# Another order of loads and first projections in the opening of a two-layer kernel

## The chip, the cores and the metric

The kernel runs on one core of one Trainium2 chip. A core has a matrix engine (TensorE, PE in the profile), three engines for elementwise work (VectorE or DVE, ScalarE or ACT, GpSimd or POOL) and a synchronisation engine (SyncE or SP) that here only issues transfers. Each engine works through its own queue strictly in order; transfers from any queue share 16 DMA engines. Time is device microseconds, from the start of the program to its end; lower is better.

## The reference

Two pre-normed transformer layers over `x` of 2 sequences, 1024 tokens each, 128 channels, all in float32:

```python
x = x + _L0_attn_ref(_layernorm(x, axis=-1), L0_attn_Wq, ..., L0_attn_proj)   # 16 heads of 64, causal
x = x + _L0_ffn_ref(_layernorm(x, axis=-1), L0_ffn_W, ...)                    # dense + one of four low ranks
x = x + _L1_attn_ref(_layernorm(x, axis=-1), L1_attn_W_k, ...)                # 16 heads of 8, distances
x = x + _L1_ffn_ref(_layernorm(x, axis=-1), L1_ffn_Wr1, ...)                  # 8 experts, 2 used, + a shared one
```

The part that matters here is the way into the first attention:

```python
xn = (x - mean) / sqrt(var + eps)                     # per token
q = einsum('bse,hde->bhsd', xn, Wq) + bq              # k and v alike
scores = where(causal, -inf, q @ k^T / 8)
z = (softmax(scores) / 8) @ v
```

## The kernel before

The whole kernel is one function, `two_layers`. The first attention is cut into 16 units, one for each pair of heads of each sequence (8 chunks of 128 weight rows, for 2 sequences). `project(unit)` gives six pieces of work for a unit: q, k and v, each for two halves of 512 tokens. It reads the normed, transposed input `xnT` and the transposed weights `wqkvT`; a piece is two matmuls 64 wide over 512 tokens (q, k), or sixteen small ones (v), and an eviction from PSUM: q on ScalarE (L407), k on VectorE (L415), v on ScalarE (L423). After that a loop runs over 128 items of one query block each: `scores`, `weigh` (softmax), `divide`, `flip` (transposes), `keep`, `attend`, and in between the projections of the next unit. In the loop the order on the engines is the one written out by hand (`manual_schedule`); ahead of it a scheduler places the instructions, within the dependences and the buffers of the pools.

What stands ahead of the loop is called the opening here. In the order of the source it is this:

- `x` is loaded in four transfers of 256 KB on SyncE's queue (L77 and L78). 512 tokens each make a quarter; the first two are sequence 0.
- Wq and Wv are loaded whole (512 KB each) on ScalarE's queue, Wk on GpSimd's (L252 to L258). GpSimd's queue also carries the biases `bnat` and `vnat`, the output projection `proj` (512 KB), and some thirty small weights of the later parts (L260 to L303).
- `layernorm_T` (L115) takes the four quarters: statistics on VectorE (L121, L122), the reciprocal root through Ln and Exp on ScalarE (L99, L100) with a refinement on VectorE (L103 to L106), the normed tokens `xn` (L128), a transpose on TensorE (L132) and a copy to `xnT` (L133).
- The 24 chunks of the weights are transposed four at a time and copied to `wqkvT` (L307 to L312), then the biases.
- `small_weights` (L328) and `sides_of_rows` (L315) prepare the weights of the later parts: transposes with copies (L140, L141), a few small matmuls, and a chain at its end that goes over `wvT`, `bd`, two selects on GpSimd (L374, L378) and `m2` (L384).
- Then the PSUM pool of the opening is closed (`early.close()`, L732), the loop's pool is opened, and the six pieces of unit 0 are put out (L736).

PSUM has eight banks, and `dealt` shares them out. In the opening `big` gets four banks, which nothing there uses, `tr` (transposes) two and `acc` (projections) two. In the loop `acc` is a single bank:

```python
early.enter_context(dealt(big=(2, 2), tr=(2, 1), acc=(2, 1)))            # L249, the opening
l0.enter_context(dealt(sc=(2, 2), flip=(1, 2), z=(1, 1), acc=(1, 1)))    # L735, the loop
for piece in project(units[0]):                                          # L736
    piece()
```

A transfer issued by an engine's queue waits for the transfer that used the same semaphore before. There are eight semaphores for SyncE and ScalarE together, given out in the order in which the scheduler places the transfers, and eight for GpSimd; so a queue may stand still until an earlier transfer has landed, and everything behind it on that engine as well.

Of the kernel before, what the change touches and what calls it, by code (L numbers as in the profile page):

```python
# [9 lines left out]
FP = mybir.dt.float32  # L10
AF = mybir.ActivationFunctionType
ALU = mybir.AluOpType
AX = mybir.AxisListType

P = 128
# [5 lines left out]
def two_layers(ctx: ExitStack, tc: tile.TileContext, a: dict, out: bass.AP):  # L21
    nc = tc.nc
    V, S, G, T = nc.vector, nc.scalar, nc.gpsimd, nc.tensor

    B, SEQ, D = a["L0_attn_x"].shape
    H, DH, _ = a["L0_attn_Wq"].shape
    NC = H * DH // P
    NB = SEQ // P
    NT = B * NB
    TOK = B * SEQ  # L30
    NG = TOK // 512
# [10 lines left out]
    xnp = ctx.enter_context(tc.tile_pool(name="xnp", bufs=2))  # L42
# [5 lines left out]
    @contextmanager  # L48
    def dealt(waits="pool", **tags):
        assert sum(n * size for n, size in tags.values()) == 8  # L50
        with tc.tile_pool(name="ps", bufs=1, space=bass.MemoryType.PSUM, reuse_waits=waits) as pool:
            banks.update(pool=pool, tags=tags)
            yield
# [8 lines left out]
    def tr():  # L62
        return bank("tr").rearrange("p o (j q) -> p (o j) q", q=P)
# [10 lines left out]

    x = const.tile([P, NT, D], FP, name="x")
    xin = a["L0_attn_x"].rearrange("b (n p) e -> p (b n) e", p=P)
    for g in range(NG):  # L77
        nc.sync.dma_start(x[:, 4 * g : 4 * g + 4, :], xin[:, 4 * g : 4 * g + 4, :])  # L78

    nc.scalar.preload_act_table_set("natural_log_exp_and_others")  # L80
    ident = const.tile([P, P], FP, name="ident")
    make_identity(nc, ident)
# [29 lines left out]
            part()  # L112


    def layernorm_T():  # L115
        xnT = xnp.tile([P, TOK], FP, tag="xnT", name="xnT")
        for g in range(NG):
            mv = small.tile([P, 4, 2], FP, tag="mv", name="mv")
            for j in range(4):
                st = small.tile([P, V.BN_STATS_DIM], FP, tag="st", name="st")  # L120
                V.bn_stats(st, x[:, 4 * g + j, :])  # L121
                V.bn_aggr(mv[:, j, :], st)  # L122
            rstd = small.tile([P, 4], FP, tag="rstd", name="rstd")
            rsqrt(rstd, mv[:, :, 1], EPS, ALU.add)
            t = tr()
            for j in range(4):
                xn = work.tile([P, D], FP, tag="xn", name="xn")
                V.tensor_scalar(  # L128
                    xn, x[:, 4 * g + j, :], mv[:, j, 0:1], rstd[:, j : j + 1],
                    ALU.subtract, ALU.mult,  # L130
                )
                T.transpose(t[:, j, :], xn, ident)  # L132
            V.tensor_copy(xnT[:, bass.ts(g, 512)], t.rearrange("p j q -> p (j q)"))  # L133
        return xnT

    def transposed(dst, src):

        n, m = src.shape
        t = tr()
        T.transpose(t[:m, 0, :n], src, ident[:n, :n])  # L140
        V.tensor_copy(dst, t[:m, 0, :n])  # L141
# [85 lines left out]
    with ExitStack() as l0:  # L227
        wp = l0.enter_context(tc.tile_pool(name="l0w", bufs=1))
        wqkvT = wp.tile([P, 3, H * DH], FP, name="wqkvT")
# [16 lines left out]
        qkv = l0.enter_context(tc.tile_pool(name="qkv", bufs=3))  # L246
        zp = l0.enter_context(tc.tile_pool(name="zp", bufs=3))
        early = l0.enter_context(ExitStack())
        early.enter_context(dealt(big=(2, 2), tr=(2, 1), acc=(2, 1)))  # L249
        stage = early.enter_context(tc.tile_pool(name="stage", bufs=1))  # L250
        nat = []
        for i, k in enumerate("qkv"):  # L252
            w = stage.tile([P, NC, D], FP, name=f"nat_{k}")
            eng = (nc.scalar, nc.gpsimd, nc.scalar)[i]
            eng.dma_start(
                w, a[f"L0_attn_W{k}"].rearrange("h d e -> (h d) e").rearrange("(c p) e -> p c e", p=P)
            )
            nat.append(w)  # L258
        bnat = stage.tile([2 * NC, P], FP, name="bnat")
        for i, k in enumerate("qk"):  # L260
            nc.gpsimd.dma_start(
                bnat[i * NC : (i + 1) * NC, :],
                a[f"L0_attn_b{k}"].rearrange("(c two) d -> c (two d)", two=2),
            )
        vnat = stage.tile([H, 2, DH], FP, name="vnat")
        for r in range(2):
            nc.gpsimd.dma_start(vnat[:, r, :], a["L0_attn_bv"])
        nc.gpsimd.dma_start(proj, a["L0_attn_proj"].rearrange("(m p) e -> p m e", p=P))


        names = {
# [3 lines left out]
        raw = {}  # L275
        for k, src in names.items():
            raw[k] = stage.tile(list(src.shape), FP, name=f"raw_{k}")
            nc.gpsimd.dma_start(raw[k], src)
        raw["wd"] = stage.tile([NR, D], FP, name="raw_wd")
        raw["wu"] = stage.tile([P, P], FP, name="raw_wu")  # L280
        G.memset(raw["wu"], 0.0)
        for i in range(4):
            r = slice(roff[i], roff[i] + ranks[i])
            nc.gpsimd.dma_start(raw["wd"][r, :], a[f"L0_ffn_Wd{i}"])
            for j in range(2):
                nc.gpsimd.dma_start(
                    raw["wu"][:, j * DH + r.start : j * DH + r.stop], a[f"L0_ffn_Wu{i}"]
                )
        simI = stage.tile([NP, 4 + NP], FP, name="simI")
        nc.gpsimd.dma_start(simI[:, :4], a["L0_ffn_sim"])  # L290
        bp = stage.tile([NP, 1], FP, name="bp")
        nc.gpsimd.dma_start(bp, a["L0_ffn_bp"].unsqueeze(1))
        temp = stage.tile([P, 1], FP, name="temp")
        nc.gpsimd.dma_start(temp, a["L0_ffn_temp"].partition_broadcast(P))
        nc.gpsimd.dma_start(wr1, a["L1_ffn_Wr1"])
        nc.gpsimd.dma_start(br1, a["L1_ffn_br1"].unsqueeze(1))
        nc.gpsimd.dma_start(wr2, a["L1_ffn_Wr2"])
# [3 lines left out]
        nc.gpsimd.dma_start(raw["be1"][NE * NF :, :], a["L1_ffn_bs1"].rearrange("(f p) -> f p", p=P))  # L301
        nc.gpsimd.dma_start(be2[:NE, :], a["L1_ffn_be2"])
        nc.gpsimd.dma_start(be2[NE:, :], a["L1_ffn_bs2"].unsqueeze(0))  # L303
        xnT = layernorm_T()
        xn2T = xnp.tile([P, TOK], FP, tag="xnT", name="xn2T")

        for i in range(3):  # L307
            for c0 in range(0, NC, 4):
                t = tr()
                for c in range(4):  # L310
                    T.transpose(t[:, c, :], nat[i][:, c0 + c, :], ident)
                V.tensor_copy(wqkvT[:, i, c0 * P : (c0 + 4) * P], t.rearrange("p j q -> p (j q)"))  # L312
        transposed(bqk, bnat)

        def sides_of_rows():  # L315

# [73 lines left out]
        def project(unit):  # L390

            b, c = divmod(unit["n"], NC)
            q = unit["q"] = qkv.tile([P, NB, 2, DH], FP, tag="q", name="q")
            k = unit["k"] = qkv.tile([P, SEQ], FP, tag="k", name="k")
            v = unit["v"] = qkv.tile([P, NB, P], FP, tag="v", name="v", bufs=4)
            cols = bass.ts(c, P)

            def heads(which, xs):
                t = acc().rearrange("p j q -> p (j q)")
                for hh in range(2):  # L400
                    hs = slice(hh * DH, (hh + 1) * DH)
                    mm(t[hs, :], wqkvT[:, which, c * P + hh * DH : c * P + (hh + 1) * DH], xs)
                return t

            def do_q(j, xs):
                t = heads(0, xs)
                S.activation(  # L407
                    q[:, 4 * j : 4 * j + 4].rearrange("p i r u -> p i u r"),
                    t.rearrange("p (i u r) -> p i u r", r=2, u=DH),
                    AF.Identity, bias=bqk[:, c : c + 1], scale=-SC,  # L410
                )

            def do_k(j, xs):
                t = heads(1, xs)
                V.tensor_scalar(k[:, bass.ts(j, 512)], t, bqk[:, NC + c : NC + c + 1], None, ALU.add)  # L415

            def do_v(j, xs):
                t = acc()
                for i in range(4):
                    for half in range(2):  # L420
                        hs = slice(half * DH, (half + 1) * DH)
                        mm(t[hs, i, :], xs[:, i * P + half * DH : i * P + (half + 1) * DH], wqkvT[:, 2, cols])
                S.copy(v[:, 4 * j : 4 * j + 4, :], t)  # L423

            out = []
            for f in (do_q, do_k, do_v):
                for j in range(SEQ // 512):
                    xs = xnT[:, b * SEQ + j * 512 : b * SEQ + (j + 1) * 512]
                    out.append(lambda f=f, j=j, xs=xs: f(j, xs))
            return out  # L430
# [289 lines left out]
        for n in range(-1, len(units)):  # L720
            for i in range(4):
                if n >= 0:
                    items.append(units[n]["items"][4 + i])
                if n + 1 < len(units):
                    items.append(units[n + 1]["items"][i])
        transposed(bz, vnat.rearrange("h r d -> h (r d)"))
        V.tensor_scalar(bz, bz, SC, None, ALU.mult)

        V.tensor_scalar(bqk[:, :NC], bqk[:, :NC], -SC, None, ALU.mult)
        small_weights()  # L730
        sides_of_rows()
        early.close()  # L732
        pp = l0.enter_context(tc.tile_pool(name="pp", bufs=3))
        tp = l0.enter_context(tc.tile_pool(name="tp", bufs=1))
        l0.enter_context(dealt(sc=(2, 2), flip=(1, 2), z=(1, 1), acc=(1, 1)))  # L735
        for piece in project(units[0]):  # L736
            piece()
        zs = bank("z")[:, 0, :]
        longs, shorts, later, ends = [], [], [], []
        LAG = 2  # L740
# [647 lines left out]
```

## Time and profile before

| what | us |
|---|---|
| median of 3 runs | 1130.3 |
| lowest, highest | 1128.53, 1133.51 |
| the profiled execution | 1134.24 |
| its span | 1132.5 |
| PE busy in the span | 1033.1 (91%) |
| VectorE, ScalarE, GpSimd busy | 591.9, 679.9, 356.6 |
| VectorE's three waits for `x` in the first 40 us | 9.0 in all |
| first matmul of the program | 14.1 |
| first projection | 39.07 |
| first scores | 50.23 |
| first projection of unit 1 | 56.47 |

The profile is of one execution. Its page has the busy time of the engines, a row of busy tenths for each engine over 40 slices of the span with the clock that TensorE was granted, the chain of work that ended last, and groups of instructions. A group's line gives the source line, engine, operation, the written and read tiles, the count, then busy time with the mean of one in ns, and the idle time before them with what ended it. A float32 matmul is shown as two passes: two matmuls of a piece are "x4". PEld is TensorE's load of the standing operand. The shares of busy time are an average over the span, so the opening has to be looked at by itself: in its timeline, in stretches of some microseconds, and in the chain.

### The profile page before, as it was taken

What the parts mean: (1) busy time and instruction counts of PE and PEld (TensorE: products, weight loads), DVE (VectorE), ACT (ScalarE), POOL (GpSimd) and SP (SyncE); (2) the same over time, 40 slices, a digit from 0 to 9 for tenths busy, and PEclk for the clock granted to TensorE, in tenths of its full rate; (3) what the DMA queues carried; (4) which work ended last, traced back from release to release, by engine and by line L of the source; (5) the groups of instructions that cost most, each with busy time, mean ns of one, the idle gap of its engine ahead of it and who ended that gap; (6) DMA issues with size and microseconds to landing.
All of it is one profiled execution on the core that took longest, in us unless ns stands there. A gap on an engine that the chain in (4) does not pass through costs nothing.

```text
span 1132.5 us, 26027 instructions
## 1 busy us (share of the span) xinstructions
PE 1033.1 (91%) x10662; PEld 624.3 (55%) x10662; DVE 591.9 (52%) x1694; ACT 679.9 (60%) x1286; POOL 356.6 (31%) x496
## 2 busy tenths in 40 slices
PE   3699999999999999999778999999999997898798
PEld 2356766766666666767555233233333235698776
DVE  5366677787878788688753324012141114464432
ACT  1176666666766656676554777888784785334351
POOL 8133334343534443444441110000104002326513
PEclk9599999999999999999999999999998898789899
DMA  5000000000000000000005000000001000112112
GB/s 125 1 1 2 2 2 2 2 2 2 2 2 2 2 2 2 2 2 2 1 2 156 13 1 1 1 1 1 19 1 29 1 1 10 54 32 70 55 37 64
DMA packets 24358, 20.12 MB, mean 18 GB/s; under 512 B 2742, under 2 KB 21520, under 8 KB 24240
## 3 DMA queue, kind: packets, MB, share of 16 engines
q1 hardware_dynamic: 18352, 10.88, 3.2%
q0 software_dynamic: 3808, 6.53, 2.2%
q8 instruction: 84, 1.38, 0.5%
q10 hardware_dynamic: 2080, 1.05, 0.4%
q14 instruction: 34, 0.28, 0.1%
HBM read 13.34 MB, written 5.11 MB: 16 GB/s over the span
## 4 chain that ended last, share of the span: by engine, by line
PE 77%; DVE 9%; ACT 6%; issue 4%; POOL 1%; another core or an unknown queue 1%; DMA 1%; SPq 0%; DVEq 0%; ACTq 0%; POOLq 0%
PE accp L69 26%; PE bigp L69 13%; PE scp L69 10%; PE zp L69 9%; PE flipp L487 7%; PE upp L69 4%; PE trp L69 3%; ACT pT L492 2%; ACT p L457 1%; DVE pT L492 1%; DVE p L453 1%; DMA x<-in_L_attn_x_dram 1%; PE trp L1125 1%; ACT hs L1265 1%
## 5 line engine op out<-in xcount | busy, mean ns | idle before, releaser
L1097 ACT ACTIVATE e<-bigp 128x1024 f32<-128x1024 f32 x256 | 247.9, 1021 | 90.5 <-PE bigp L69 79.0
L469 POOL TENSOR_SCALAR p<-p,rz 128x128 f32<-128x128 f32 (+7 forms) x256 | 187.7, 746 | 305.5 <-DVE rz L466 270.8
L457 ACT ACTIVATE p<-p,nmax 128x128 f32<-128x128 f32 (+7 forms) x256 | 196.3, 769 | 25.1 <-DVE nmax L453 24.4
L453 DVE CUSTOM_DVE_ANT_0 p<-scp,mask 128x128 f32<-128x128 f32 (+7 forms) x256 | 183.4, 754 | 34.9 <-PE scp L69 24.6
L492 ACT COPY pT<-flipp 128x128 f32<-128x128 f32 (+7 forms) x128 | 81.3, 636 | 152.2 <-PE flipp L487 147.3
L69 PE MATMUL bigp<-rT,lT 32*128 32x512 f32 x1024 | 162.2, 649 | 4.8 <-ACT e L1097 4.4
L69 PE MATMUL scp<-k,q 64*128 64x512 f32 (+3 forms) x768 | 164.0, 509 | 0.0
L69 PEld LDWEIGHTS zp<-pT,v 128*64 128x64 f32 x2560 | 137.4, 138 | 26.2 <-issue 7.1
L69 PE MATMUL zp<-pT,v 128*64 128x128 f32 (+1 forms) x2560 | 147.3, 266 | 1.4 <-DVE zT L516 0.7
L487 PEld LDWEIGHTS flipp<-ident,p 64*128 64x128 f32 x2304 | 92.8, 140 | 98.6 <-issue 48.7
L69 PE MATMUL accp<-e,own 128*32 128x512 f32 x1024 | 141.4, 614 | 0.0
L487 PE MATMUL flipp<-ident,p 64*128 64x64 f32 x2304 | 112.0, 230 | 19.8 <-DVE rz L466 11.8
L492 DVE COPY pT<-flipp 128x128 f32<-128x128 f32 (+7 forms) x128 | 96.1, 751 | 59.0 <-PE flipp L487 59.0
L69 PEld LDWEIGHTS bigp<-rT,lT 32*128 32x128 f32 x1024 | 51.6, 185 | 115.4 <-issue 71.0
L973 POOL DMA_INDIRECT xs<-rows,from x46 | 46.9, 1020 | 189.2 <-PE trp L1245 87.6
L1265 ACT ACTIVATE hs<-upp,w 128x128 f32<-128x128 f32 x184 | 51.9, 371 | 73.9 <-issue 59.2
L69 PEld LDWEIGHTS scp<-k,q 64*128 64x128 f32 x768 | 70.0, 192 | 39.1 <-issue 34.2
L69 PE MATMUL accp<-xnT,wqkvT 128*64 128x512 f32 x256 | 72.5, 647 | 7.2 <-ACT q L407 2.8
L1114 DVE COPY cs<-accp 128x512 f32<-128x512 f32 x16 | 11.0, 690 | 105.4 <-PE accp L69 105.4
L69 PE MATMUL accp<-w,hs 128*128 128x128 f32 x368 | 54.7, 296 | 11.3 <-ACT hs L1265 8.6
L69 PE MATMUL upp<-xsT,w 128*128 128x128 f32 x368 | 56.4, 304 | 4.1 <-DVE xsT L1247 4.1
L69 PEld LDWEIGHTS accp<-e,own 128*32 128x32 f32 x1024 | 21.0, 108 | 68.7 <-issue 66.1
(313 smaller groups left out, 1152.5 us busy)
## 6 DMA issues: line engine op xcount, KB each, us to landing
given<-y SPq DMA_DIRECT2D x10, 256.0 KB, 2.3
wx<-in_L_ffn_We_dram SPq DMA_DIRECT2D x1, 2048.0 KB, 8.7
wx<-in_L_ffn_We_dram SPq DMA_DIRECT2D x8, 256.0 KB, 5.1
x<-in_L_attn_x_dram SPq DMA_DIRECT2D x4, 256.0 KB, 4.0
rows<-xn SPq DMA_DIRECT2D x4, 256.0 KB
out_dram<-out SPq DMA_DIRECT2D x4, 256.0 KB
xs<-rows,from POOLq DMA_INDIRECT x46
nat_q<-in_L_attn_Wq_dram ACTq DMA_DIRECT2D x1, 512.0 KB
```

The lines of the kernel that those rows point to most:

```text
L69: T.matmul(o, lhsT=lhsT, rhs=rhs, start=start, stop=stop)
L453: V.tensor_tensor_reduce(out=p[:, :n], in0=it["sc"][hh], in1=mask[:, SEQ - n :], scale=1.0, scalar=-NEG, op0=ALU.add, op1=ALU.min, accum_o ...
L457: S.activation(p[:, :n], p[:, :n], AF.Exp, bias=nmax, scale=-1.0, accum_out=it["sum"][:, hh : hh + 1],)
L469: G.tensor_scalar(p[:, :n], p[:, :n], r[:, hh : hh + 1], SC, ALU.mult, ALU.mult)
L487: T.transpose(it["t", hh][:, r, j, :], it["p"][hh][rs, bass.ts(j, P)], ident[rs, rs])
L492: copy(it["group"]["pT", hh][:, : i + 1, i % 2].rearrange("p j r u -> p r j u"), it["t", hh])
L973: G.indirect_dma_start(out=xs[:, j, :], out_offset=None, in_=rows[b][:, :], in_offset=bass.IndirectOffsetOnAxis(ap=r["from"][:, 4 * q + j ...
L1097: S.activation(e[:, 2 * pr : 2 * pr + 2, :], sc[pr], AF.Exp, scale=1.0 / math.sqrt(DK))
L1114: V.tensor_copy(cs, state["c"])
L1125: T.transpose(t[:, j, :], cs[:, j, :], ident)
L1265: S.activation(h[:, f, :], t[:, f, :], AF.Silu, bias=w[:, I + NF * D + f : I + NF * D + f + 1])
```

## The change

The opening gets another order. Of `x` only sequence 0 is issued first. On ScalarE's queue stand the first chunk (64 KB) of Wq, Wk and Wv, then the two bias rows, then the remaining seven chunks of Wq and Wv; the second half of `x` and the rest of Wk go out from SyncE. `proj` and most of the small weights move from GpSimd's queue to SyncE's. PSUM in the opening is dealt as four `tr` and four `acc` buffers. The first chunk of all three weights is transposed into one tile and copied with one instruction; after it come the norms of sequence 0, the six pieces of unit 0, the norms of sequence 1, the other 21 chunks (in groups of four and three), the bias of v, `small_weights` and `sides_of_rows`. The loop follows straight on.

```diff
-    for g in range(NG):
-        nc.sync.dma_start(x[:, 4 * g : 4 * g + 4, :], xin[:, 4 * g : 4 * g + 4, :])
+    def load_x(b):
+        for g in range(b * NG // B, (b + 1) * NG // B):
+            nc.sync.dma_start(x[:, 4 * g : 4 * g + 4, :], xin[:, 4 * g : 4 * g + 4, :])
+    load_x(0)
...
-    def layernorm_T():
-        xnT = xnp.tile([P, TOK], FP, tag="xnT", name="xnT")
-        for g in range(NG):
+    def layernorm_T(b):
+        for g in range(b * NG // B, (b + 1) * NG // B):
...
-        early.enter_context(dealt(big=(2, 2), tr=(2, 1), acc=(2, 1)))
+        early.enter_context(dealt(tr=(4, 1), acc=(4, 1)))
...
-            eng = (nc.scalar, nc.gpsimd, nc.scalar)[i]
-            eng.dma_start(
-                w, a[f"L0_attn_W{k}"].rearrange("h d e -> (h d) e").rearrange("(c p) e -> p c e", p=P)
-            )
+        def load_nat(eng, i, cs):
+            w = a[f"L0_attn_W{'qkv'[i]}"].rearrange("h d e -> (h d) e").rearrange("(c p) e -> p c e", p=P)
+            eng.dma_start(nat[i][:, cs, :], w[:, cs, :])
+        for i in range(3):
+            load_nat(nc.scalar, i, slice(0, 1))
...
-            nc.gpsimd.dma_start(
+            nc.scalar.dma_start(
                 bnat[i * NC : (i + 1) * NC, :],
...
+        load_x(1)
+        load_nat(nc.scalar, 0, slice(1, NC))
+        load_nat(nc.sync, 1, slice(1, NC))
+        load_nat(nc.scalar, 2, slice(1, NC))
...
-        nc.gpsimd.dma_start(proj, a["L0_attn_proj"].rearrange("(m p) e -> p m e", p=P))
+        nc.sync.dma_start(proj, a["L0_attn_proj"].rearrange("(m p) e -> p m e", p=P))
...
-            nc.gpsimd.dma_start(raw[k], src)
+            nc.sync.dma_start(raw[k], src)
...
-            nc.gpsimd.dma_start(raw["wd"][r, :], a[f"L0_ffn_Wd{i}"])
+            nc.sync.dma_start(raw["wd"][r, :], a[f"L0_ffn_Wd{i}"])
...
-        nc.gpsimd.dma_start(simI[:, :4], a["L0_ffn_sim"])
+        nc.sync.dma_start(simI[:, :4], a["L0_ffn_sim"])
...
+        def turn_nat(*which):
+            t, at = tr(), 0
+            for i, cs in which:
+                for c in cs:
+                    T.transpose(t[:, at, :], nat[i][:, c, :], ident)
+                    at += 1
+            i, cs = which[0]
+            if len(which) == 1:
+                dst = wqkvT[:, i, cs[0] * P : (cs[-1] + 1) * P]
+                V.tensor_copy(dst, t[:, :at, :].rearrange("p j q -> p (j q)"))
+            else:
+                V.tensor_copy(wqkvT[:, :, cs[0] * P : (cs[0] + 1) * P], t[:, :at, :])
...
+        turn_nat(*[(i, [0]) for i in range(3)])
+        transposed(bqk, bnat)
+        V.tensor_scalar(bqk[:, :NC], bqk[:, :NC], -SC, None, ALU.mult)
+        layernorm_T(0)
+        for piece in project(units[0]):
+            piece()
+        layernorm_T(1)
+        for i in range(3):
+            for cs in (range(1, 5), range(5, NC)):
+                turn_nat((i, cs))
         transposed(bz, vnat.rearrange("h r d -> h (r d)"))
...
         small_weights()
         sides_of_rows()
         early.close()
...
-        for piece in project(units[0]):
-            piece()
```

The `raw["wu"]` parts, `bp` and `temp` move to SyncE's queue in the same way; the two loads of `vnat` and those of the second layer's router and biases stay on GpSimd's.

## Prediction

> **What bounds the kernel now.** I read the page first: busy shares, then the span in 40 slices (28.3 us each), where the question is which slices are not full.
>
> ```profile
> PE   3699999999999999999778999999999997898798
> ...
> PEclk9599999999999999999999999999998898789899
> ```
>
> TensorE (PE) is full from the third slice on. Only the opening, 0 to about 57 us, leaves it at 3 and 6 tenths, and there the granted clock falls to 5. So what the change can win or lose lies in some 57 us; behind them a shift of the start is a shift of the end. The second view is the chain of work that ended last, cut to the first 60 us (start, duration, piece):
>
> ```profile
> 1.83 10.54 DMA x<-in_L_attn_x_dram
> 12.39 0.29 DVE st L121
> ...
> 38.72 0.30 DVE m L384
> 39.07 2.00 PE accp L69 x4
> 41.09 1.15 ACT q L407
> 42.29 2.00 PE accp L69 x4
> ...
> 55.83 0.59 ACT v L423
> 56.47 2.00 PE accp L69 x4
> ```
>
> To be seen: over ten microseconds of waiting for x; then norms, transposes and small weights to 39.07; then unit 0's six projections one after the other, each with the eviction of its single accumulator behind it, to 56.47. In that last stretch PE works at half clock, which the third view (stretches; granted clock is the third number from the right) dates:
>
> ```profile
> 33.00:34.00 1.00, 0.83 (x4) 0.67 (x4) 0.49 (x5) 0.41 (x2) 0.00 (x0) 0.67 0.00 0
> ...
> 60.00:61.00 1.00, 1.00 (x4) 0.00 (x0) 0.41 (x4) 0.90 (x3) 0.00 (x0) 0.67 0.00 0
> ```
>
> 0.67 in one microsecond is a change after a third and after two thirds of it: down at 33.34, up at 60.66. The rows before 33 say 1.00, but durations disagree:
>
> ```profile
> L311 PE MATMUL trp<-ident,nat_q 128*128 128x128 f32 x8 | 2.6, 428 | 0.6 <-DVE wqkvT L312 0.6
> L311 PE MATMUL trp<-ident,nat_v 128*128 128x128 f32 x8 | 1.3, 286 | 0.2 <-DVE wqkvT L312 0.2
> ```
>
> The same transpose took 428 ns at 22.9 to 26 us and 286 ns from 27.7 on: I take PE as slow until about 26 us, whatever the column says.
>
> **The change, step by step**, by the order in which the built program places instructions on each engine; durations from the rows and the timeline of before.
>
> 1. *Transfers.* The stretches (last two numbers: DMA share, GB/s):
>
> ```profile
> 0.00:5.00 5.00, 0.00 (x0) 0.00 (x0) 0.42 (x3) 1.28 (x1) 4.29 (x22) 1.00 0.52 143
> 5.00:10.00 5.00, 0.00 (x0) 0.00 (x0) 2.11 (x16) 0.41 (x2) 3.81 (x7) 1.00 1.19 296
> 10.00:15.00 5.00, 0.89 (x3) 0.55 (x3) 2.61 (x20) 0.41 (x2) 3.01 (x7) 1.00 0.93 249
> ```
>
> When x's third quarter arrived at 12.39, 0.72 + 1.48 + 0.60 = 2.8 MB had moved, 0.79 MB of it x: Wq, Wk, Wv and proj share the engines. Now ahead of x's end there are 1.05 MB of x and 0.2 MB of first chunks: 5 + (1.25 - 0.72)/0.296 = 6.8 us, about 7.3 landed. ACT's queue: bk waits for x's second quarter (about 5.3) to free its semaphore; behind it stand the rests of Wq and Wv (0.49 and 0.61 to issue) and then the norms' Ln, free at about 7.0; before, the first Ln ran at 7.86. The other 2.1 MB land by 7.3 + 2.1/0.296 = 14.4, long before use.
>
> 2. *VectorE (DVE).* All 16 statistics stand ahead of the first refinement. A quarter took 1.15 to 1.25 us when packed: from 4.4 to 9.4, so x no longer sets the pace. Twelve refinements in interleaved threes at 0.09: 10.5. Then three xn (0.82), the new 384-wide weight copy (between 0.28 for 128 and 0.69 for 512: 0.55), bqk (0.16 + 0.2), three xn (1.0), xnT (0.69): 13.9. Before, the first xnT copy ended at 17.57.
>
> 3. *Unit 0's projections* start there instead of at 39.07. Four accumulators replace one, so only PE counts: the first piece 2.0 and four to six transposes at 0.42 to 17.5; then five pieces, 2.0 each at half clock, 1.08 at full (the row at 62.49: four passes in 1.08). All slow: 27.5; all fast: 22.9. Between them the clock decides, and here trace and rule differ. In the trace the duration fell near 26.5 us behind transposes alone (428 to 286 ns), and the two changes of the column lie 60.66 - 33.34 = 27.3 us apart. The Trainium skill, "TensorE: Matmul & The Clock Gate", says in Part 1 that a free-running window of about 3.4 us has to be busy before the clock doubles (eight such windows make 27.3, so the trace agrees), and in Part 4 that transposes do not count as busy in the same way (here they seem to). By the rule only the stretch from 17.5 counts: fast between 20.9 and 24.3, end about 25.1. By the row the stretch from 13.9 counts: end about 23.4. The half-empty start makes me choose 24.5.
>
> 4. *Second sequence and the other weights.* PE first ends unit 0, then two xn transposes (0.6). DVE is the longer: two xnT copies 0.69, three xn 0.34, three copies of 512 at 0.69, three of 384 at 0.55 = 6.1: 31.2. Before, with two PSUM buffers instead of four, seven copies took 5.5.
>
> 5. *Small weights.* The same work; before it took from 29.91 to 39.07 = 9.2. VectorE's own durations up to wvT add up to 3.4, plus 0.4 of waiting for colscale's Ln and Exp; from wvT on the chain is fixed: matmul 0.83, bd 0.3, two selects on GpSimd 0.9, matmul 0.8, m2 0.3, semaphores 0.3 = 3.4. Sum 7.2 (side_of, 0.68 in the old path, is done earlier): 38.4. At full clock the two matmuls would save 0.8.
>
> 6. *The loop.* First scores at 38.5, its projection of unit 1 0.8 behind them. Before, that projection began at 56.47, so the loop's equivalent start was 55.67. Gain 55.7 - 38.5 = **17.2 us**. Behind that the order on all engines is the same. The loop starts at half clock in both: before it was released 4.2 us after 56.47; now a 3.4 us window ends 3.4 to 6.8 after 38.5, so 2.6 to 6.0 after the like point: at most 1 us either way.
>
> *GpSimd* loses 24 of 34 issues, some 13 us of its queue; the masks and `own` come earlier, nobody waits. *SP* gets 22 more; nothing else stands on it until 607 us. But each waits for the transfer eight back, and sim is third from the end. The trace shows no tiny transfer on SP. Rows near: GpSimd 0.51 to 0.58 each, back to back with the same eight-back wait, so landing within 4.4 us; SP 0.43 to 0.97 for 256 KB. Below 0.43 I see no reason. From about 14 (proj lands) eleven steps of 0.6 and a landing of 2 (an estimate from the 2.3 of `given`): sim at 22.6. VectorE asks for it (simsq) behind k's second eviction at about 22, and it next needs PE at about 24.5, so up to 1.8 us late costs nothing. I take 0.6 and no cost; at 1.0 sim lands at 27.0 and costs 2.5.
>
> **Sum.** The profiled execution took 1134.24 us (span 1132.5), 3.9 over the median of 1130.3 (1128.53 to 1133.51). 1134.2 - 17.2 = 1117.0 for it; against the median 1130.3 - 17.2 = **1113 us**.
>
> **Rivals.**
> - *The opening fills less than I add up (0.15).* PE stays slow through all projections (27.5, +3) and sim comes late (+3, partly in the same wait): start at 42 to 45, gain 11 to 14, time about 1118. For it: the clock stayed at half from 34 to 60 in stretches that were 60 to 85% busy. Against: then each matmul stood behind an eviction; four accumulators remove that.
> - *Small transfers on SP become the bound (0.05): slower.* VectorE is strictly in order, and behind simsq stand xnT's second half, all weight copies and small weights. If each transfer costs what a lone one costs instead of overlapping, sim lands at 14 + 12p. The stall begins above p = 0.9 and eats the whole gain when sim is 17.2 later than 24.5, at p = 2.3; at p = 2.8 the time is 1136. The Trainium skill, "DMA: Bandwidth & Descriptors", Anatomy of one DMA, gives about 2.0 us fixed per transfer (for GpSimd's path): serially that would land sim near 38 and leave 4 us of gain, 1126. The GpSimd row speaks against: 0.55 per step with the same wait.
> - *x was not the delay (0.05).* If landing is set by something else than the sharing, x's last quarter still comes after 12 us, all steps move by 4 and the gain is 13: 1117.
> - *The change does not reach the end of the loop:* excluded nearly, since PE is at 9 tenths from 60 us and no order changes there; a rest of 0.05 for no change.
>
> **How the numbers follow.** My case 0.70, 1113, from 1109 (start at 35.5: clock high throughout, the skew of 1 us) to 1117. The next cases reach 1119, so the range is 1108 to 1120 with run scatter of 2. What can be told from no change here is about 0.5%, 5.7 us: all cases but the SP stall and the last are beyond it. Faster 0.90, within 0.05, slower 0.05.
>
> **What would show it.** Right: first scores near 38.5; the first `accp<-xnT,wqkvT` near 14; statistics without a wait for x after 8 us; no wait of simsq on a DMA; one stretch of half clock at the loop's start that ends within 7 us. Wrong: a wait of VectorE on `simI`, a first Ln after 9, unit 0's projections ending after 27, or a first score after 45.

## The result and the profile after

| | before | after |
|---|---|---|
| median (4 runs each) | 1129.78 | 1117.84 |
| lowest, highest | 1128.53, 1133.51 | 1115.91, 1119.32 |
| the profiled execution | 1134.24 | 1117.2 |
| its span | 1132.5 | 1115.5 |
| first projection of unit 0 | 39.07 | 17.60 |
| first scores | 50.23 | 40.29 |
| first projection of unit 1 | 56.47 | 41.02 |

Times in us. The ratio to the kernel before is 0.9853, 95% interval 0.9819 to 0.9888. The two medians by themselves give 0.9894, just above that interval; in a second set (last section of the experiments) they give 0.9847 with a ratio of 0.9855, interval 0.9821 to 0.989. Single runs of either kernel scatter by several microseconds, so below the stages are compared by their starts in the trace.

The page of the changed kernel, rows of 40 slices (28 us each); the first two slices are the opening:

```profile
PE   5899999999999999998779999999998997887897
...
PEclk9799999999999999999889999999998999899799
```

PE has gone from 3 and 6 tenths to 5 and 8, the clock's low from 5 to 7. Behind the second slice the rows are nearly those of before. The chain of waits of the changed kernel, first 45 us (start, duration, piece):

```profile
1.29 3.98 DMA x<-in_L_attn_x_dram
...
9.39 0.22 DVE rsq L107 x3
9.61 3.96 DVE rsq L108 x3
13.57 0.20 DVE rstd L109 x3
13.77 1.72 DVE xn L130 x3
...
16.88 0.69 DVE xnT L135
17.56 0.04 issue
17.60 1.97 PE accp L69 x2
...
22.71 4.63 PE accp L69 x44
...
40.29 0.80 PE scp L69 x4
41.09 1.93 PE accp L69 x4
```

The 10.54 us of waiting for x are 3.98, and from 5.29 on VectorE works without a gap, as forecast. But three tiny operations, a step of the norms' refinement on 128x4 values (L108), stand on the chain with 3.96 us, where the three of the step ahead took 0.22. The first xnT copy, which opens the projections, ends at 17.55, the same as before (17.57), and not at 13.9.

The timeline shows what stood beside them. A row with x3 runs from the start of the first to the end of the last of three; and an instruction's record begins before the one ahead of it has ended, so that a row behind a stalled one looks long as well (rstd below ends 0.2 behind rsq). VectorE, then GpSimd of the changed kernel (start, duration, engine, line):

```profile
9.31 0.30 DVE L107 TENSOR_TENSOR rsq<-rsq,rstd 128x4 f32<-128x4 f32 x3
9.53 4.04 DVE L108 TENSOR_SCALAR rsq<-rsq 128x4 f32<-128x4 f32 x3
9.75 4.02 DVE L109 TENSOR_TENSOR rstd<-rstd,rsq 128x4 f32<-128x4 f32 x3
13.68 1.81 DVE L130 TENSOR_SCALAR xn<-x,mv,rstd 128x128 f32<-128x128 f32 x3
```

```profile
9.61 0.51 POOL L311 DMA_DIRECT2D be<-in_L_ffn_bs_dram  x1 [0.88 <-DMA vnat<-in_L_attn_bv_dram]
10.11 0.54 POOL L332 MEMSET row<- 128x512 f32 x1
10.57 2.46 POOL L171 MEMSET own<- 128x2816 f32 x1
12.95 0.35 POOL L337 MEMSET row<- 128x32 f32 x6
13.21 0.33 POOL L172 MEMSET own<- 128x128 f32 x1
13.62 1.27 POOL L339 TENSOR_TENSOR row<-row,ident 128x512 f32<-128x512 f32 x1
```

VectorE comes free at 13.57, 0.03 behind the end of the last memset (13.21 + 0.33), and the three xn take 1.81 in place of 0.82 beside GpSimd's multiplication. Of the three rsq the first two took 0.16 each; the third began at 9.67, while GpSimd was still issuing its last transfer and 0.43 before the first memset by its record. Experiment 2 has the same issue without the clearing behind it.

The same three before the change (xn by the timeline, the memset's two uses in the program with their first and last start, the copies with their mean of 692 ns):

```profile
13.65 0.82 DVE L128 TENSOR_SCALAR xn<-x,mv,rstd 128x128 f32<-128x128 f32 x3
...
L170 POOL MEMSET own<- x2: 2449/2461/2473, 26.4 to 607.5; 128x2816 f32 x2
...
L312 DVE COPY wqkvT<-trp 128x512 f32<-128x512 f32 x6 | 4.0, 692 | 1.8 <-PE trp L311 1.5
```

There the large memset began at 26.4, because GpSimd still had transfers to issue; it ran beside copies out of PSUM, which kept their 0.69 each. Taking the issues from GpSimd moved its clearing of `own` and `row` up by 16 us, onto the norms.

### The profile page after: what moved, and what is told of

Same layout as the page of the kernel before. It is cut to its first block, busy times and chain, and to the rows that moved or that the text cites. A ratio compares the mean times of both kernels' runs of the same rounds, so it can differ in the third digit from the quotient of the medians.

```text
span 1115.5 us, 26029 instructions
## 1 busy us (share of the span) xinstructions
PE 1026.0 (92%) x10662; PEld 620.1 (56%) x10662; DVE 595.6 (53%) x1695; ACT 680.4 (61%) x1286; POOL 345.1 (31%) x472
## 3 DMA queue, kind: packets, MB, share of 16 engines
q8 instruction: 84, 1.38, 0.5%
## 4 chain that ended last, share of the span: by engine, by line
PE 78%; DVE 10%; ACT 6%; issue 5%; POOL 1%; another core or an unknown queue 0%; DMA 0%; DVEq 0%; SPq 0%; POOLq 0%; ACTq 0%
PE accp L69 27%; PE bigp L69 13%; PE scp L69 11%; PE zp L69 9%; PE flipp L501 8%; PE upp L69 4%; PE trp L69 3%; ACT pT L506 2%; ACT p L471 1%; DVE pT L506 1%; DVE p L467 1%; PE trp L1146 1%; DVE rsq L106 1%; DVE rsq L107 1%; PE trp L197 1%
## 5 line engine op out<-in xcount | busy, mean ns | idle before, releaser
L69 PEld LDWEIGHTS zp<-pT,v 128*64 128x64 f32 x2560 | 137.9, 138 | 26.4 <-issue 7.1
L69 PE MATMUL accp<-w,hs 128*128 128x128 f32 x368 | 56.0, 301 | 14.4 <-ACT hs L1286 7.9
L69 PEld LDWEIGHTS accp<-w,hs 128*128 128x128 f32 x368 | 51.3, 212 | 16.6 <-ACT hs L1286 8.7
```

Source lines behind the costliest of these rows:

```text
L69: T.matmul(o, lhsT=lhsT, rhs=rhs, start=start, stop=stop)
```

## The experiments

From the trace there were two theories for the stall: GpSimd's clearing and VectorE's small SBUF operations exclude each other; or the transfers, at 280 GB/s from 9 to 14.4 us, slow VectorE.

**1. `own` cleared in the loop.**

```diff
-        fill(own[0], G)
         n = 0
...
                 divide(items[n - 1])
+            if n == 1:
+                fill(own[0], G)
```

> The memset of own (2.46 + 0.33 us on GpSimd at 10.57 in the changed kernel) moves behind the first piece of the loop; the memsets of row and its add with ident stay. Theory (GpSimd's memsets and VectorE's small SBUF-to-SBUF operations exclude each other): VectorE's stall of about 4.0 us at 9.5 falls to 1 to 1.7 us, the first xnT copy ends at 14.5 to 15.2 in place of 17.55, the first scores come at 37.3 to 38.2 in place of 40.3. Rival (VectorE was slowed by the transfers that run at full rate until 14.4): the stall is unchanged, first xnT copy 17.5, first scores 40.3. Time 1114.5 to 1116 by the theory, 1117.8 by the rival, each within the scatter of 2.

Timeline of VectorE, then of GpSimd, in this kernel:

```profile
9.95 0.90 DVE L108 TENSOR_SCALAR rsq<-rsq 128x4 f32<-128x4 f32 x3
10.87 0.31 DVE L109 TENSOR_TENSOR rstd<-rstd,rsq 128x4 f32<-128x4 f32 x3
11.09 1.80 DVE L130 TENSOR_SCALAR xn<-x,mv,rstd 128x128 f32<-128x128 f32 x3
```

```profile
10.26 0.54 POOL L332 MEMSET row<- 128x512 f32 x1
10.86 0.33 POOL L337 MEMSET row<- 128x32 f32 x6
11.27 1.28 POOL L339 TENSOR_TENSOR row<-row,ident 128x512 f32<-128x512 f32 x1
```

What is left of the stall lies exactly beside what is left of the clearing: rsq until `row`'s memset is over, xn until its multiplication is. rstd, with two inputs in SBUF, runs undisturbed beside six small memsets. The copy ends at 14.95, first scores come at 36.10, 1.2 sooner than my theory's earliest: the clock rose 2.5 us after the projections began here, and 5.4 after in the changed kernel. In the 3.4 us before the rise PE was busy for 3.22 us (the first number behind the length), 1.97 of them with projections, the rest with transposes:

```profile
14.11:17.53 3.42, 3.22 (x8) 0.91 (x7) 2.15 (x10) 0.00 (x0) 0.00 (x0) 1.00 0.17 27
```

One run took 1110.6.

**2. `row` late as well**, on top of experiment 1. It is zeroed by multiplying a part of unit 0's q by 0, so that GpSimd has to wait for it.

```diff
-            G.memset(row, 0.0)
+            G.tensor_scalar(
+                row.rearrange("p k h j -> p (k h j)"), units[0]["q"][:, :4].rearrange("p i r u -> p (i r u)"),
+                0.0, None, ALU.mult,
+            )
```

> own is zeroed in the loop as in the first experiment, and row is zeroed by an operation that reads unit 0's q, so that all of GpSimd's clearing waits until VectorE has done the first transposes' copies. Theory: all of the 4.9 us goes: the rsq and rstd steps take 0.15 to 0.2 us each, xn 0.82 for three, first xnT copy ends at 12.6 to 13.9, first scores at 35.4 to 36.8; time about 1113. Rival (the transfers slow VectorE): first xnT copy still at about 17.5, first scores 40.3, time 1117.8. A third way: the clearing of row now lies beside the second half's xn and its stall comes back there; then first xnT near 13 but first scores no earlier than 39.

Timeline of VectorE, and a stretch of 1 us with engines, clock, DMA share and GB/s:

```profile
9.92 0.30 DVE L108 TENSOR_SCALAR rsq<-rsq 128x4 f32<-128x4 f32 x3
10.13 0.29 DVE L109 TENSOR_TENSOR rstd<-rstd,rsq 128x4 f32<-128x4 f32 x3
10.35 0.85 DVE L130 TENSOR_SCALAR xn<-x,mv,rstd 128x128 f32<-128x128 f32 x3
```

```profile
10.00:11.00 1.00, 0.26 (x1) 0.19 (x2) 1.00 (x9) 0.05 (x1) 0.41 (x1) 1.00 1.19 303
```

The stall is gone with 303 GB/s moving beside it (295 in the same microsecond of the changed kernel), so the transfers are not its cause. Nor is GpSimd's issue of its last transfer, which stands here at 9.90 to 10.41, beside the same rsq. The copy ends at 13.26, first scores at 35.60; one run took 1110.1. Between these, 1.7 us of earlier projections than in experiment 1 bought 0.5: experiment 8 goes into that.

**3. Two accumulators** in place of four for unit 0 (and six transposing buffers).

```diff
-        early.enter_context(dealt(tr=(4, 1), acc=(4, 1)))
+        early.enter_context(dealt(tr=(6, 1), acc=(2, 1)))
```

> Two accumulators in place of four for unit 0's projections, and six transposing buffers in place of four. The prediction's step 3 takes it that with four accumulators only PE counts. With two accumulators each piece needs the eviction of the piece before the last (ACT 1.0 to 1.2 us against 2.0 us of PE at half clock): if that is so, two are enough as well, the projections end at 27.3 plus or minus 0.7 and the first scores come at 40.3 plus or minus 0.7. Rival (the four accumulators carry the gain of this stage): the projections end 2 to 4 us later, first scores at 42 to 44.

Projections end at 27.68, first scores at 39.67 (27.34 and 40.29 with four); one wait of 0.30 for an eviction. The ends alone don't compare, since the clock rose 2.3 us after the projections began here, and 5.4 after with four; the wait does. More than two bring next to nothing here; a single one was not tried in this order.

**4. The small weights back on GpSimd's queue**, x, proj and the large weights as changed.

```diff
-            nc.sync.dma_start(raw[k], src)
+            nc.gpsimd.dma_start(raw[k], src)
```

and the same for `wd`, `wu`, `sim`, `bp` and `temp`.

> The small weights' transfers go back from SP to GpSimd's queue; proj and the rests of Wq, Wk, Wv stay where the change put them. GpSimd then has some 22 more issues ahead of its memsets, at 0.5 to 0.6 us each, so the memsets come at 20 us or later. Theory (memsets against VectorE): the stall at 9.5 to 13.6 is gone, the first xnT copy ends at 12.7 to 14.5, first scores at 36 to 39 unless sim, now behind GpSimd's issues, comes late. Rival (the full-rate transfers slow VectorE): first xnT copy at 17.5, first scores 40 or later.

The stall at 9.5 is gone (copy ends at 12.71) but it comes again further back, where the clearing now falls into the second half's norms. The copy out of PSUM stands behind the stalled xn in VectorE's queue and ends 0.02 after it. VectorE, then GpSimd:

```profile
22.78 3.27 DVE L130 TENSOR_SCALAR xn<-x,mv,rstd 128x128 f32<-128x128 f32 x1 [1.24 <-PE trp L134]
23.05 3.02 DVE L135 COPY xnT<-trp 128x512 f32<-128x512 f32 x1
```

```profile
23.00 2.46 POOL L171 MEMSET own<- 128x2816 f32 x1
25.39 0.35 POOL L337 MEMSET row<- 128x32 f32 x6
25.64 0.33 POOL L172 MEMSET own<- 128x128 f32 x1
```

First scores at 38.38: still 1.9 sooner than with these transfers on SyncE. With the clearing where it stood, that part of the change lost time. One run took 1113.0.

**5 and 6. The change cut in two**: transfers as before with the new computing order, and the new transfers with the old computing order (projections behind the small weights, PSUM dealt as before). Diff of the first, in its core:

```diff
     load_x(0)
+    load_x(1)
...
-            load_nat(nc.scalar, i, slice(0, 1))
+            load_nat((nc.scalar, nc.gpsimd, nc.scalar)[i], i, slice(0, NC))
```

with `bnat`, `proj` and the small weights on GpSimd; and of the second:

```diff
-        early.enter_context(dealt(tr=(4, 1), acc=(4, 1)))
+        early.enter_context(dealt(big=(2, 2), tr=(2, 1), acc=(2, 1)))
...
         zs = bank("z")[:, 0, :]
+        for piece in project(units[0]):
+            piece()
```

> All transfers on the queues and in the order of the kernel before, the computing in the changed order. Theory: x's last quarter comes at about 14 again and the 16 statistics wait for it, so the first xnT copy ends at 18 to 20; but GpSimd has its 34 issues again, so its memsets lie beyond 25 us and VectorE has no stall at 9.5: the late x and the memsets cost about the same. First scores at 41 to 44, the projection of unit 1 at 42 to 45: nearly all of the gain over the kernel before (56.5) is there without any change of a transfer. Rival (the transfers carry a good part of the gain): first scores at 48 or later.

> All transfers as changed, the computing in the order of the kernel before (unit 0's projections behind the small weights, one accumulator). Theory: the early x is eaten by the memsets of GpSimd, which come early too: VectorE stalls 4 to 5 us from about 9.5, the first xnT copy ends at 15.5 to 18, and unit 1's projection begins at 53.5 to 57 (before 56.5): gain 0 to 3. Rival (earlier transfers help by themselves, as the prediction's x landing at 7.3 in place of 13.9 has it): unit 1's projection at 49 to 51.

Unit 1's projection began at 42.15 with the new computing alone (one run: 1117.0) and at 56.97 with the new transfers alone (1138.2; the kernel before was at 1131.7 beside it, and its single runs range from 1127.66 to 1139.15), against 56.47 before. In the second the stall is there again (VectorE, then GpSimd):

```profile
9.89 3.64 DVE L99 TENSOR_SCALAR rsq<-mv 128x4 f32<-128x4 f32 x1
9.97 3.57 DVE L106 TENSOR_TENSOR rsq<-rsq,rstd 128x4 f32<-128x4 f32 x3
13.59 1.38 DVE L107 TENSOR_TENSOR rsq<-rsq,rstd 128x4 f32<-128x4 f32 x3
```

```profile
13.59 1.30 POOL L339 TENSOR_TENSOR row<-row,ident 128x512 f32<-128x512 f32 x1
```

And the first shows what does not stall: the two k evictions, from PSUM, beside the large memset (mean 0.75, as without it); VectorE, then GpSimd:

```profile
25.78 1.61 DVE L426 TENSOR_SCALAR k<-accp,bqk 128x512 f32<-128x512 f32 x2 [1.38 <-PE accp L69]
```

```profile
26.25 2.48 POOL L172 MEMSET own<- 128x2816 f32 x1
```

**7. PE kept busy in the small weights**, on top of experiment 2: matmuls that nobody reads are added, with three accumulators in place of four to make room for them.

```diff
+        def busy(n, w=512):
+            for _ in range(n):
+                mm(idle[:, :w], ident, wqkvT[:, 0, :w])
...
                 transposed(dst, raw[k])
+                busy(1, 256)
...
             mm(t[:, 0, :], wvT, wkT)
+            for _ in range(4):
+                mm(idle[:, :P], wvT, wkT)
```

> Built on the second experiment (all of GpSimd's clearing late): matmuls whose result nobody reads are added into a PSUM bank of their own between the small weights' steps (five of 256 or 512 columns, four of 128), three accumulators in place of four. It adds work only. In the second experiment the clock fell at 31.3, with PE some 60% busy from 27.5, and rose at 41.9, 6.3 us after the first scores. Theory (the half clock at the loop's start costs 2 to 3 us and is owed to PE's idling in the small weights): the clock stays at 1.00 or is back by 37, the small weights end 0.5 to 1 us sooner or no later, a like point at 60 to 100 us comes 2 to 3.5 us sooner. Rival 1 (the added matmuls stand in the way and the clock falls all the same): first scores 0.5 to 2 us later. Rival 2 (the loop's start is not bound by PE): clock up, but the like point at 60 us within 0.7 of the second experiment's.

First scores at 37.19, 1.6 later. Two stretches of experiment 2, then two of this one (the granted clock is the third number from the right):

```profile
31.00:32.00 1.00, 0.86 (x4) 0.49 (x4) 0.66 (x5) 0.32 (x3) 0.00 (x0) 0.83 0.00 0
41.00:42.00 1.00, 1.00 (x8) 0.54 (x8) 0.02 (x1) 0.47 (x2) 0.49 (x2) 0.55 0.00 0
```

```profile
35.00:36.00 1.00, 0.78 (x6) 0.48 (x4) 0.74 (x3) 0.00 (x0) 0.80 (x2) 0.56 0.00 0
41.00:42.00 1.00, 0.90 (x4) 0.29 (x4) 0.78 (x4) 0.54 (x3) 1.00 (x1) 0.52 0.00 0
```

A mean of 0.83 is a fall at 31.66, 0.56 one at 35.12; both rise at 41.9. The clock fell 3.4 us later and the end of the slow stretch did not move; the added matmuls cost more than that brought. At the first squaring of `own` the kernel is 1.0 behind (512.48 against 511.45). The first rival holds: the added matmuls stand in the way and the clock falls all the same. What a loop that starts at full clock would gain stays open.

**8. `row` out of the path altogether.** `own` is cleared late as in experiment 2; `row` is again cleared by a memset, but in the loop, in a part of another tile that is not yet used. In experiment 2 the chain ran from the first q eviction over GpSimd's `row` to VectorE's side_of, with the next xn behind it.

```diff
-            row = stage.tile([P, 4, 4, 32], FP, name="row")
+            row = xn2T[:, TOK - 512 :].rearrange("p (k h j) -> p k h j", k=4, j=32)
...
-            V.tensor_reduce(side_of, row, AX.X, ALU.add)
+            return lambda: V.tensor_reduce(side_of, row, AX.X, ALU.add)
...
+            if n == 2:
+                sides = sides_of_rows()
+            if n == 4:
+                sides()
```

> Built on the second experiment, whose chain of waits runs through row: VectorE stood 1.46 us at 20.9 for GpSimd's row before its own side_of, with the next xn behind it. Here own is cleared in the loop's second step, row's work comes in the third (in a stretch of xn2T that is not yet used), and side_of in the fifth, where it is not needed before 500 us. Theory: VectorE goes through to the second k eviction and xn at about 22.2 in place of 23.8; first scores at 34.1 to 35.0 in place of 35.6 to 36.0; the loop loses at most 0.5 by VectorE's 0.7. Rival (the projections' end on PE at 22.8 holds the second half anyway, and the clock's steps of 3.4 us swallow what is left): first scores within 0.4 of 35.8. Median 1110 to 1113 in either case, the scatter being as large as the difference.

First scores at 35.41 (experiment 2: 35.60, and 35.11 in a run beside this one). The second k eviction does end at 21.6 in place of 23.8, but the next xn waits until 22.88 for PE, whose projections end at 22.59. The rival, that PE holds the second half anyway, fits.

**The changed kernel and two variants, timed together**, six runs each:

> The changed kernel once more, beside the two variants on the same chip: 1116 to 1119.5 by its own four runs; first scores within 0.3 of 40.3, VectorE's stall of 4.0 us at 9.5 again.

> The first experiment's kernel (own zeroed in the loop), timed. Theory: the loop starts 4.2 us sooner than the changed kernel's and nothing gives it back, so the median is 3 to 6 us below the changed kernel's, 1111 to 1115. Rival (what is won in the opening is lost again where the clock falls late in the kernel): less than 2 us below it.

> The second experiment's kernel (own and row both cleared late), timed. Theory: 4.7 us of earlier start, median 3.5 to 6.5 us below the changed kernel's, and 0 to 1 below the first experiment's, which the scatter hides. Rival: less than 2 us below the changed kernel's.

| | median | lowest, highest | ratio to before | first scores |
|---|---|---|---|---|
| before (11 runs) | 1136.14 | 1127.66, 1139.15 | | |
| changed | 1118.75 | 1116.36, 1123.81 | 0.9855 (0.9821 to 0.989) | 39.77 |
| `own` late | 1114.11 | 1112.12, 1116.36 | 0.9815 (0.9783 to 0.9847) | 35.97 |
| `own` and `row` late | 1111.83 | 1108.93, 1115.23 | 0.9785 (0.9752 to 0.9818) | 35.95 |

The stall came again in the changed kernel (3.52 us at 10.22, and 1.38 for the three rstd beside GpSimd's multiplication); its first scores came 0.5 sooner than in the first profile, where 0.3 had been allowed. With it removed the median falls by 4.6 and 6.9 us; the ranges of the changed kernel and of the last variant do not overlap. A third set gave the last variant (first scores at 35.11, where 35.6 to 36.0 had been expected) 1111.5 (0.9803, 0.9766 to 0.9841) and experiment 8 1113.71 (0.9822, 0.979 to 0.9855), which can't be told apart. The version with both late beats both kernels.

## Why the prediction came out as it did

The steps side by side, in us of the profiled executions:

| step | predicted | changed | both late (exp. 2) |
|---|---|---|---|
| VectorE's statistics done | 9.4 | 9.0 | 9.4 |
| first xnT copy ends | 13.9 | 17.55 | 13.26 |
| unit 0's projections end | 24.5 | 27.34 | 22.76 |
| second half's copies end | 31.2 | 32.99 | 28.98 |
| first scores | 38.5 | 40.29 | 35.60 |
| unit 1's projection, against 56.47 | -17.2 | -15.45 | -20.1 |

- **The step that failed** is the cost put at nothing: "*GpSimd* loses 24 of 34 issues, some 13 us of its queue; the masks and `own` come earlier, nobody waits." VectorE waited 3.75 us for it in the refinement (3.96 less some 0.2) and 1.0 in xn (1.81 less 0.82). I counted the DMA issues that left a queue and not what moves up behind them. Two of the prediction's own signs said so: the first projection came at 17.60 and not near 14, and unit 0's projections ended after 27. The chain that step 2 added up for VectorE was right (13.26 where the clearing is late), and only 0.6 too long. The Trainium skill, "SBUF — State Buffer", section "Who interferes with whom", has the rule: VectorE and GpSimd share one port pair, and the one that is first holds it for a whole instruction against copies and tensor_scalar in the modes that use both ports of VectorE, and against operations with two inputs in SBUF where GpSimd reads SBUF. Every row above agrees, the undisturbed rstd beside the small memsets too; that copies and evictions out of PSUM go on beside a memset is what the runs show (0.69 and 0.75 each). Which of the two was first can't be read from the records (the third rsq's start lies ahead of the first memset's), and that the port is what they share is the page's word: the runs show which pairs of operations exclude each other. GpSimd's operations stood back to back, and VectorE didn't get in between until 13.57.
- **Two terms were too long and hid half of it.** From the first copy the projections took 9.8 us (10.6 predicted), the second half 5.65 (6.7). 3.65 late, less 0.8 and 1.05, leaves 1.8 at the first scores. That they offset half of the delay is luck; and the first rival's time, about 1118, fits as well as the forecast's, though not its start at 42 to 45. A total that is near is no proof of its terms.
- **Transfers (step 1)** did what was forecast: one wait of 3.0 for x, the first Ln at 6.68, no wait at simsq; on SyncE the tiny transfers took 0.25 to 0.49 each to issue (0.6 taken; sim issued at 19.04), so the slower rival was far off. But they were not where the gain was. Unit 1's projection went from 56.47 to 42.15 by the computing order alone (experiment 5), to 39.11 with x, proj and the large weights loaded as changed (experiment 4), back to 41.02 with the small weights on SyncE, and to 36.33 with the clearing late. With the old computing order the transfers bring nothing (56.97). These steps hold in the order in which they are added, each from one trace; the first scores of experiment 2's kernel lay at 35.11 to 35.95 in three. The small weights on GpSimd's queue with the clearing late were not run, so that SyncE by itself costs anything is not shown.
- **The clock (steps 3 and 6).** It was fast from 23.0. The prediction's 17.5 is the moment behind the first piece and its transposes; in the run that moment is 22.71 (chain above), and the rule counted from there gives 26.1 to 29.5. Counted with the transposes, as the row has it, from the first piece at 17.60, it gives 21.0 to 24.4, and that holds. Experiment 1 agrees: the clock rose 2.5 us after the first piece, less than a window, so the transposes ahead of and behind the piece counted. This is also why 10.6 was too long: 24.5 was chosen between the two readings, and the row's 23.4 lies 9.5 behind the first copy, which is what experiment 2 took. In the loop the clock was back 5.9 us after unit 1's projection (2.6 to 6.0 predicted behind the like point).
- **From the trace to the median.** The profiled spans differ by 17.0, the starts of the loop by 15.45, the first squaring of `own` by 14.8 (531.0 to 516.2). The rest arises behind that, in code that didn't change: 1.6 up to the last `accp<-e,own`, and from the last `accp<-e,own` to the end of the span it took 192.0 before, 191.4 after, and 188.5 to 195.9 in the experiments, with dips of the clock at different places. So it is luck that the profiled execution came out at 1117.2 where 1117.0 was forecast for it. The forecast from the median, 1113, is 4.8 below 1117.84; by the runs the clearing accounts for 4.6 to 6.9 us, and the two over-long terms took some back.

## What to carry to other kernels

Work that is taken off a queue lets everything behind it start sooner, also what was harmless where it stood: list what moves up, on which engine, and beside what. Clearing on GpSimd belongs beside work of VectorE that reads PSUM, and away from short SBUF-to-SBUF steps on the critical path, where a jump of a group's mean (rsq of line 108: 908 ns, 161 before) gives the collision away. A change of several parts wants each part run alone: here one brought 14.3 us, one 3.0, and one, as the clearing stood, lost 1.9.

## What was not expected of the hardware

The clock changes only on a grid. In every kernel here the slow stretch at the loop's start is a multiple of 3.41 us within 0.05: 27.3 before and in experiment 6, 13.7 after, 10.2 in experiments 1 to 5, 6.8 in experiment 7, 13.7 in experiment 8. Its place against the work differs by run, and so can its length with one and the same kernel: the changed kernel had 10.2 in its second profile, and experiment 2's 13.7 in its second and 10.2 in its third. At the loop's start it rose only behind a step in which PE was busy for 97% or more; of the changed kernel's last two slow steps, the first with 3.19 of 3.41 us did not do it:

```profile
40.07:43.48 3.41, 3.19 (x10) 1.33 (x12) 0.74 (x6) 1.32 (x5) 0.72 (x2) 0.50 0.00 0
43.48:46.89 3.41, 3.32 (x14) 1.01 (x12) 1.01 (x6) 2.43 (x6) 0.00 (x1) 0.50 0.00 0
```

The first rise of all took less: 83% before the change (2.84 of 3.41 us, transposes alone) and 94% in experiment 1, so no single threshold can be read from these runs. Where the work falls on this grid is worth up to a step: experiment 2 began its projections 1.7 us before experiment 1 and had the fast clock 0.5 later (18.0 and 17.5). What makes it fall isn't settled: in experiment 4 a step of 48% busy left it up, in experiment 7 one of 76% took it down.
